# Two input transposes of a four-layer graph network moved from TensorE to VectorE blocks and DRAM, with a new instruction order

## The chip, the cores and the metric

The kernel runs on one core of a Trainium2 chip. The time is device microseconds of one execution; a run is compared with the kernel before on the same chip in the same rounds. The record marks an execution as slow when it is over 1.5% above the fastest of its kernel. In the lines of the profile PE is TensorE, PEld its weight loads, DVE VectorE, ACT ScalarE, POOL GpSimd and SP SyncE, whose queue (SPq) issues the DMAs; L480 is line 480 of that run's kernel, `x8` a count of instructions, and `<-` in brackets names what ended the wait before.

## The reference

The input is 32 graphs of 512 nodes with 256 features in fp32, and one 512 x 512 adjacency matrix shared by all. Four layers follow each other; each is `x = layernorm(x + layer(x))`.

```python
def reference(x, adj, ...):
    x = ln(x + L0(x))   # 8-head attention over adj, layernorm, FFN with relu, layernorm
    x = ln(x + L1(x))   # additive attention: softmax(leaky_relu(s1_i + s2_j) masked) @ (x W)
    x = ln(x + L2(x))   # softmax(leaky_relu((x W1)(x W2)^T) masked) @ (x W3), relu
    x = ln(x + L3(x))   # additive attention with 4 heads, elu
    return x            # ... cut: parameters, masks, constants
```

## The kernel before

A planner in the kernel's own Python decides the order of all instructions. Each operation has an assumed cost per engine; the planner starts what can start first and breaks ties by the age of the graph and the length of the work behind the operation. Every engine then executes its own list strictly in that order, so an instruction whose input is late holds everything behind it on its engine.

```python
AGE = 30.0
...
s, o, e = min((c for c in cands if c[0] <= tmin + 0.05),
              key=lambda c: (not c[1].frees, c[1].graph * AGE - c[1].rank))
...
plan = Plan(slots, {...}, 5, {"DVE": 1.0})      # five graphs in flight
```

The FFN of layer 0 and layer 2 need their input with features on the partitions. `transposed` did that on TensorE, eight 128 x 128 transposes into PSUM (the buffers that matmuls write, `ps` in the traces), copied out ("evicted") by ScalarE:

```python
def transposed(xs):
    xT = Buf("B")
    for s in range(2):
        ps = Buf("PS")
        def fn(e, s=s, ps=ps):
            for k in range(KC):
                for j in range(2):
                    nc.tensor.transpose(two(ps)[:, k, j * P:(j + 1) * P],
                                        T4(xs)[:, 2 * s + j, k * P:(k + 1) * P], ident)
        op({"PE": 4 * TR}, fn, r=[xs[s]], w=[ps], pre=[xT])
        evac(ps, xT, s, nodes(s), two)
    return xT
```

A layernorm works on half a graph at a time: statistics on VectorE, then four tiny steps on GpSimd (two columns each), then the scaling of the data on ScalarE:

```python
def layernorm(y, dst, ...):
    for s in halves:
        ...                                            # bn_stats, bn_aggr on VectorE -> mv
        def scales(e, mv=mv):
            m = mv.t[:, :4].rearrange("p (c k) -> p k c", k=2)
            nc.gpsimd.tensor_scalar(mv.t[:, 4:6], m[:, 1, :], 1.0, EPS, ALU.mult, ALU.add)
            nc.gpsimd.tensor_tensor(mv.t[:, 6:8], mv.t[:, 4:6], mhalf[:, :2], ALU.pow)
            nc.gpsimd.tensor_scalar(mv.t[:, 8:10], m[:, 0, :], -1.0, 0.0, ALU.mult, ALU.add)
            nc.gpsimd.tensor_tensor(mv.t[:, 10:12], mv.t[:, 8:10], mv.t[:, 6:8], ALU.mult)
        op({"POOL": 1.6}, scales, r=[mv], w=[mv])      # the planner assumes 1.6 us
        ...                                            # norm: ScalarE, x * scale + bias
```

## Time and profile before

| | before |
|---|---|
| median of the first 3 runs | 3023.44 us (3019.70 to 3026.94) |
| span of the trace | 3020.5 us |
| steady period per graph | 90.44 us, TensorE without a gap |
| span minus 32 periods (both ends) | 126.4 us |
| VectorE, ScalarE, DMA busy in a period | 81.7 us, 52.5 us, 12% |

The steady period is the distance of two equal instructions of neighbouring graphs in the trace. What is left of the span after 32 periods is what filling, draining and setup cost; I call it "the ends". The prediction shows the lines.

### The profile page before, as it was taken

The numbers are of one execution on the slowest core, as the hardware profiler recorded it, in microseconds if no ns is written. First come the engines' busy times: TensorE is split into PE (matmuls) and PEld (weight loads), VectorE is DVE, ScalarE is ACT, GpSimd is POOL, SyncE is SP. The second block draws the span as 40 slices with busy tenths as digits, with TensorE's granted clock in tenths as the row PEclk, the third lists the DMA queues.
The fourth block names the chain that finished last, engine by engine and source line by source line (L and its number), as shares of the span: only waits on it lengthen the run. The fifth ranks groups of instructions, "written<-read, shape, count | busy, mean of one in ns | idle before, by whom it ended". The sixth has DMA issues, their size and how long they took to land.

```text
span 3020.5 us, 49063 instructions
## 1 busy us (share of the span) xinstructions
PE 2947.4 (98%) x17898; PEld 1633.3 (54%) x17898; DVE 2635.2 (87%) x5277; ACT 1688.5 (56%) x3475; POOL 866.8 (29%) x1809
## 2 busy tenths in 40 slices
PE   8999999999999999999999999999999999999885
PEld 3465555555555555555555555555555555555452
DVE  7988899988899988899988899988899988889754
ACT  5546655665655665555665555665555665655432
POOL 0223322322322322322322322322322322322221
PEclk9999999999999999999999999999999999999997
DMA  7000110111110110110110110110110111110000
GB/s 139 12 19 22 39 39 19 40 39 22 39 39 19 39 40 22 39 39 18 40 40 22 39 39 19 40 39 22 39 39 19 40 39 24 37 32 19 32 25 29
DMA packets 194746, 102.67 MB, mean 34 GB/s; under 512 B 143937, under 2 KB 181313, under 8 KB 194497
## 3 DMA queue, kind: packets, MB, share of 16 engines
q1 hardware_dynamic: 193648, 97.63, 12.9%
q8 instruction: 142, 2.33, 0.3%
q10 hardware_dynamic: 848, 1.84, 0.2%
q14 instruction: 108, 0.88, 0.1%
HBM read 82.31 MB, written 17.12 MB: 33 GB/s over the span
## 4 chain that ended last, share of the span: by engine, by line
PE 92%; DVE 4%; issue 1%; DMA 1%; ACT 1%; POOL 1%; SPq 1%; DVEq 0%; ACTq 0%; POOLq 0%
PE ps L380 15%; PE ps L397 11%; PE ps L467 9%; PE ps L475 8%; PE ps L611 8%; PE ps L765 7%; PE ps L730 7%; PE ps L703 7%; PE ps L670 7%; PE ps L771 4%; PE ps L368 2%; PE ps L722 2%; PE ps L536 1%; PE ps L701 1%; PE ps L802 1%
## 5 line engine op out<-in xcount | busy, mean ns | idle before, releaser
L340 ACT ACTIVATE b<-ps 128x512 f32<-128x512 f32 x772 | 434.9, 602 | 497.2 <-PE ps L380 186.9
L486 DVE TENSOR_TENSOR b<-b,maskT 128x1024 f32<-128x1024 f32 x512 | 594.5, 1212 | 25.1 <-ACT b L480 25.1
L480 ACT ACTIVATE b<-ps 128x512 f32<-128x512 f32 x1024 | 528.4, 604 | 116.7 <-PE ps L475 116.7
L439 ACT ACTIVATE b<-b,t 128x256 f32<-128x256 f32 x768 | 425.6, 597 | 255.9 <-POOL t L430 244.3
L427 POOL TENSOR_SCALAR t<-t 128x2 f32<-128x2 f32 x384 | 135.2, 352 | 845.0 <-DVE t L422 777.8
L757 DVE SCALAR_TENSOR_TENSOR b<-b,s,maskT 128x512 f32<-128x512 f32 x512 | 358.7, 740 | 8.0 <-DMA b<-r 7.7
L428 POOL TENSOR_TENSOR t<-t,mhalf 128x2 f32<-128x2 f32 x384 | 340.0, 885 | 32.0
L475 PE MATMUL ps<-b,b 32*128 32x512 f32 x2048 | 300.4, 640 | 0.0
L498 DVE TENSOR_TENSOR b<-b,b 128x1024 f32<-128x1024 f32 x256 | 297.4, 1210 | 0.0
L420 DVE BATCH_NORM_STATS2 t<-b 128x6 f32<-128x256 f32 x768 | 284.4, 412 | 7.8 <-DVE b L580 0.5
L408 POOL TENSOR_TENSOR acc<-acc,s 128x32 f32<-128x32 f32 (+2 forms) x96 | 77.3, 806 | 637.8 <-DVE s L525 378.1
L467 PE MATMUL ps<-b,b 128*32 128x512 f32 x2048 | 250.9, 598 | 2.6 <-DVE b L486 2.3
L765 PE MATMUL ps<-b,b 128*64 128x512 f32 x1024 | 239.3, 606 | 13.1 <-DVE b L757 13.1
L380 PE MATMUL ps<-b,wqkv_sb 128*128 128x512 f32 x512 | 248.1, 609 | 0.0
L397 PE MATMUL ps<-w_sb,b 128*128 128x256 f32 x1024 | 245.6, 388 | 1.4 <-ACT b L340 1.4
L703 PE MATMUL ps<-b,b 128*128 128x512 f32 x512 | 240.6, 592 | 0.0
L380 PE MATMUL ps<-b,w_sb 128*128 128x512 f32 x512 | 235.5, 603 | 2.5 <-ACT b L340 2.5
L670 PE MATMUL ps<-b,b 128*128 128x257 f32 x1024 | 230.8, 383 | 2.5 <-issue 2.5
L730 PE MATMUL ps<-b,b 128*128 128x257 f32 x1024 | 228.5, 380 | 0.4 <-ACT b L340 0.4
L670 PEld LDWEIGHTS ps<-b,b 128*128 128x128 f32 x1024 | 195.8, 192 | 45.4 <-issue 10.6
L397 PEld LDWEIGHTS ps<-w_sb,b 128*128 128x128 f32 x1024 | 190.0, 191 | 53.8 <-issue 30.0
L408 POOL TENSOR_TENSOR acc<-acc,t 128x2 f32<-128x2 f32 (+2 forms) x128 | 37.9, 308 | 598.7 <-DVE t L789 325.7
(124 smaller groups left out, 4129.8 us busy)
## 6 DMA issues: line engine op xcount, KB each, us to landing
b<-r SPq DMA_DIRECT2D x64, 512.0 KB
b<-in_x_dram SPq DMA_DIRECT2D x128, 128.0 KB
b<-in_x_dram SPq DMA_DIRECT2D x32, 512.0 KB
out_dram<-b SPq DMA_DIRECT2D x64, 256.0 KB
b<-r SPq DMA_DIRECT2D x32, 256.0 KB
r<-s SPq DMA_DIRECT2D x128, 0.5 KB
r<-s SPq DMA_DIRECT2D x128, 2.0 KB
b<-in_adj_dram ACTq DMA_DIRECT2D x4, 256.0 KB
```

What stands on the lines that cost most here:

```text
L340: nc.scalar.activation(dst, src, AF.Copy)
L380: nc.tensor.matmul(ps.t, w.t[:, i, col + k * P:col + (k + 1) * P], T2(xT)[:, i, :], start=(i == 0), stop=(i == KC - 1))
L397: nc.tensor.matmul(two(ps)[:, j, :], T2(xT)[:, i, c * P:(c + 1) * P], w.t[:, i, col:col + C], start=(i == 0 and row is None), stop=(i == K ...
L439: nc.scalar.activation(o, i, AF.Identity, bias=b, scale=sc)
L467: nc.tensor.matmul(ps.t[D0 * h:D0 * h + D0, :], lhs(h), T2(p[h // 2][c])[:, h % 2, :], start=start, stop=stop)
L475: nc.tensor.matmul(s[h].t, T2(kT)[r:r + D0, g, c * P:(c + 1) * P], T2(qT)[r:r + D0, g, :], start=True, stop=True)
L480: op({"ACT": cact(512)}, lambda e, c=c, j=j, i=i, s=s, p=p: nc.scalar.activation(T2(p[j][c])[:, i, :], s[2 * j + i].t, AF.Exp, scale=SC0), ...
L486: nc.vector.tensor_tensor(t, t, maskT[c].t.unsqueeze(1).to_broadcast([P, 2, N]), ALU.mult)
L670: nc.tensor.matmul(ps.t[:, :C + 1], T2(p[m // 2])[:, m % 2, c * P:(c + 1) * P], hv.t[:, m * (C + 1):(m + 1) * (C + 1)], start=(m == 0), st ...
L703: nc.tensor.matmul(ps.t, T2(gT)[:, i, c * P:(c + 1) * P], T2(xT)[:, i, :], start=False, stop=(i == KC - 1))
L730: nc.tensor.matmul(ps_o.t[:, :C + 1], T2(pT)[:, j, m * P:(m + 1) * P], vv()[:, m, :], start=(m == 0), stop=(m == NC - 1))
L765: nc.tensor.matmul(ps_o[h // 2].t[D3 * (h % 2):D3 * (h % 2 + 1), :], T4(hv)[:, m + i, h * D3:(h + 1) * D3], T2(p[i][h // 2])[:, h % 2, :], ...
```

## The change

The intent is to take 16 transposes per graph off TensorE, the bounding engine. VectorE transposes 32 x 32 blocks, the half-done tile goes to DRAM in one write of 512 KB, and four reads of 128 KB bring the blocks back in their places. Because this takes longer, six graphs are kept in flight, the age step falls from 30 to 15, and the last two graphs get equal rank. The core of the diff:

```diff
-AGE = 30.0
+AGE = 15.0
+LAST = 2
...
-                          key=lambda c: (not c[1].frees, c[1].graph * AGE - c[1].rank))
+                          key=lambda c: (not c[1].frees, min(c[1].graph, len(self.graphs) - LAST) * AGE - c[1].rank))
...
-    plan = Plan(slots, {...}, 5,
+    plan = Plan(slots, {..., "E": [1] * 4, ...}, 6,
...
+    def quarters(xs):
+        xt = Buf("B")
+        for s in range(2):
+            op(TH, lambda e, s=s: nc.vector.transpose(
+                xt.t[:, :NC * C].rearrange("p (q c b) -> p c q b", c=NC, b=32)[:, 2 * s:2 * s + 2],
+                by_chunk(xs, s).rearrange("p c (q a) -> p c q a", a=32)),
+                r=[xs[s]], w=[xt[s]])
+        return xt
     def transposed(xs):
-        ... (TensorE transposes and evictions, shown above)
+        xt, xT, d = quarters(xs), Buf("B"), Buf("E")
+        op({"SP": DMA}, lambda e: nc.sync.dma_start(d.t, xt.t[:, :NC * C]), r=[xt], w=[d])
+        def get(e):
+            v = d.t.rearrange("(j a) (k i n) -> i a k j n", a=32, i=4, n=P)
+            for i in range(4):
+                nc.sync.dma_start(T2(xT)[32 * i:32 * i + 32].rearrange(
+                    "a k (j n) -> a k j n", n=P), v[i])
+        op({"SP": 4 * DMA}, get, r=[d], w=[xT])
         return xT
```

(The permuted node order is undone where the FFN's relu and layer 2's first product are evicted; layers 1 and 3 use `quarters` too, two half-tile transposes for four quarter-tile ones.)

More of the change, by code (lines that the diff above doesn't have):

```diff
@@ L291 @@
         "D": [tc.dram_tile([H3, N], FP, name=f"r{i}") for i in range(6)],
+        "E": [tc.dram_tile([P, NC * C], FP, name=f"e{i}") for i in range(6)],
         "PS": [psum.tile([P, N], FP, name=f"ps{i}") for i in range(8)],
@@ L297 @@
     nc.gpsimd.memset(ones, 1.0)
-    plan = Plan(slots, {"B": [14, 10, 10, 12], "S": [4] * 4, "T": [8] * 4, "D": [1] * 4, "PS": [0] * 4}, 5,
+    plan = Plan(slots, {"B": [14, 10, 10, 12], "S": [4] * 4, "T": [8] * 4, "D": [1] * 4, "E": [1] * 4, "PS": [0] * 4}, 6,
                 {"DVE": 1.0})
@@ L345, in evac @@
            r=[ps], w=[dst[part]])
-    def nodes(s):
-        return lambda b: T2(b)[:, :, s * 2 * P:(s + 1) * 2 * P]
     def swap(v):
@@ L357, in parts4 @@
         return v.rearrange("p (q i b) -> p q i b", q=NC, i=4)
-    def transposed(xs):
-        xT = Buf("B")
-        for s in range(2):
-            ps = Buf("PS")
-            def fn(e, s=s, ps=ps):
-                for k in range(KC):
-                    for j in range(2):
-                        nc.tensor.transpose(two(ps)[:, k, j * P:(j + 1) * P],
-                                            T4(xs)[:, 2 * s + j, k * P:(k + 1) * P], ident)
-            op({"PE": 4 * TR}, fn, r=[xs[s]], w=[ps], pre=[xT])
-            evac(ps, xT, s, nodes(s), two)
+    def quarters(xs):
[6 more added lines that the diff above has]
+        return xt
+    def transposed(xs):
+        xt, xT, d = quarters(xs), Buf("B"), Buf("E")
[6 more added lines that the diff above has]
+        op({"SP": 4 * DMA}, get, r=[d], w=[xT])
         return xT
@@ L383, in project_t, with project @@
         return ps
-    def project(xT, w, col, s, pre, row=None, part=None):
+    def project(xT, w, col, s, pre, row=None):
         ps = Buf("PS")
@@ L399, in fn @@
                                      stop=(i == KC - 1 and (row is None or j == 1)))
-        op({"PE": 2 * F + (0.1 if row is None else 0.33)}, fn, r=[xT[part], w] + ([row] if row else []),
+        op({"PE": 2 * F + (0.1 if row is None else 0.33)}, fn, r=[xT, w] + ([row] if row else []),
            w=[ps], pre=[pre])
@@ L560, in relu @@
             def relu(e, k=k, ps_h=ps_h):
-                o, i, b = T2(hT)[:, k, :], ps_h.t, b1_sb.t[:, k:k + 1]
+                o, i, b = swap(T2(hT)[:, k, :]), parts4(ps_h.t), b1_sb.t[:, k:k + 1]
                 if e == "ACT":
@@ L593, in scored @@
         R = [Buf("B") for _ in range(1 + (heads > 2))]
-        xt = Buf("B")
-        def xq():
-            return xt.t[:, :NC * C].rearrange("p (q c b) -> p c q b", c=NC, b=32)
-        for s in range(2):
-            for c in (2 * s, 2 * s + 1):
-                op({"DVE": cdve(256)}, lambda e, c=c: nc.vector.transpose(
-                    xq()[:, c], T4(xs)[:, c, :].rearrange("p (q a) -> p q a", a=32)),
-                    r=[xs[s]], w=[xt[s]])
+        xt = quarters(xs)
         pss = [Buf("PS") for _ in range(NC)]
@@ L685, in layer2 @@
         for k in range(KC):
-            evac(project_t(w12_sb, 0, xT, k, gT), gT, k, lambda b, k=k: T2(b)[:, k, :])
+            evac(project_t(w12_sb, 0, xT, k, gT), gT, k, lambda b, k=k: swap(T2(b)[:, k, :]),
+                 lambda b: parts4(b.t))
         def vv():
@@ L690, in layer2 @@
         for s in range(2):
-            evac(project(xT, w3_sb, 0, s, v, part=s), v, s, lambda b, s=s: vv()[:, 2 * s:2 * s + 2, :C], two)
+            evac(project(xT, w3_sb, 0, s, v), v, s, lambda b, s=s: vv()[:, 2 * s:2 * s + 2, :C], two)
         op({"DVE": 0.08}, lambda e: nc.vector.memset(vv()[:, :, C:C + 1], 1.0), r=[xT], w=[v])
@@ L859, in masks @@
             op({"DVE": 0.6}, lambda e, c=c: nc.vector.tensor_scalar(
-                swap(maskN.t[:, c, :]), parts4(edges(c)), 0.0, -BIG, ALU.is_le, ALU.mult),
+                maskN.t[:, c, :], edges(c), 0.0, -BIG, ALU.is_le, ALU.mult),
                 r=[f[c // 2][c % 2]], w=[maskN])
```

## The prediction

> **What bounds the kernel now.** I read the page first: busy shares, the 40 slices, the chain.
>
> ```profile
> PE 2947.4 (98%) x17898; PEld 1633.3 (54%) x17898; DVE 2635.2 (87%) x5277; ACT 1688.5 (56%) x3475; POOL 866.8 (29%) x1809
> ...
> PE   8999999999999999999999999999999999999885
> ...
> DVE  7988899988899988899988899988899988889754
> ...
> PE 92%; DVE 4%; issue 1%; DMA 1%; ACT 1%; POOL 1%; SPq 1%; DVEq 0%; ACTq 0%; POOLq 0%
> ```
>
> PE is busy almost everywhere, and 92% of the chain that ended last is PE. Gaps are only in the first and the last few slices. VectorE is second at 87%, and it too runs at 8 or 9 tenths for most of the program. Busy matmuls may still be stretched by waits, so I checked the rhythm. In the chain in order of time each layer-1 projection begins 90.44 us after the one before (1008.56, 1099.00, 1189.44 us), once per graph. The table of busy time by stretch over such a period:
>
> ```profile
> 1005.00:1095.44 90.44, 90.44 (x562) 50.15 (x558) 81.70 (x164) 52.48 (x109) 27.30 (x55) 1.00 0.12 33
> ```
>
> The columns are span, then busy time of PE, weight loads, VectorE, ScalarE and GpSimd, then clock, DMA share and GB/s. PE has no idle time in this period at clock 1.00, VectorE has 8.74 us of slack, DMA is 12% used. So in the middle the time is PE's work: 90.44 us per graph. 32 x 90.44 = 2894.1 us; the span is 3020.5, so 126.4 us are lost at head and tail (setup, filling, draining, slow clock). The last stretches of the same view:
>
> ```profile
> 2900.00:2960.00 60.00, 51.97 (x281) 31.80 (x274) 29.35 (x75) 21.29 (x47) 8.37 (x26) 0.91 0.09 32
> 2960.00:3020.50 60.50, 26.01 (x155) 12.55 (x153) 24.42 (x60) 8.40 (x19) 5.73 (x20) 0.74 0.09 28
> ```
>
> In the last 60 us PE works 26 us, at a clock of 0.74: the last graph runs layer 3 alone, its steps waiting for each other.
>
> **What the Trainium skill says.** (1) "VectorE: DVE Perf Modes", section The three transpose paths: VectorE transposes only 32x32 blocks, TensorE a full 128x128 into PSUM. That is why the change needs the trip through DRAM to regroup the blocks, and why the old path needs an eviction. The trace has both kinds: the block transposes of layer 0's input, and 128x128 TensorE transposes followed by ScalarE evictions. (2) "TensorE: Matmul & The Clock Gate", section PE-mode transpose, gives about 275 ns for a transpose in a kernel. The trace agrees (median 273 ns), but that is latency; transposes overlap, and the cost is their spacing, taken below. (3) "DMA: Bandwidth & Descriptors", section Anatomy of one DMA: about 2 us fixed plus bytes over 436 GB/s, fitted on another issuing path. For 512 KB that gives an estimate of 3.2 us each way. The trace before has no such round trip. Its 1 MB of loads for a new graph (issued from 1079.4 us) moved until about 1086 us at 140 to 230 GB/s in most microseconds, so I allow more. (4) "Perfetto Trace Analysis", section Identifying the Most-Contended Engine, warns that matmul busy time does not say how near PE is to its limit. It does not undo the argument here: what matters is that PE has no gap, and that removed instructions give back their spacing.
>
> **The change part by part.**
>
> *Removed from PE.* `transposed` is called twice per graph (FFN and layer 2), 8 transposes each: 16 per graph, 512 in all, which the groups view confirms:
>
> ```profile
> L368 PE MATMUL ps<-ident,b 128*128 128x128 f32 x512 | 71.8, 280 | 9.6 <-ACT b L439 9.5
> ```
>
> 512 x 280 ns would be 143 us, far too much, since they overlap. The timeline of PE in one period shows the true cost as the start of the group to the start of the next:
>
> ```profile
> 1046.39 1.03 PE L368 MATMUL ps<-ident,b 128*128 128x128 f32 x8
> 1047.36 1.14 PE L475 MATMUL ps<-b,b 32*128 32x512 f32 x8
> ...
> 1061.22 1.09 PE L368 MATMUL ps<-ident,b 128*128 128x128 f32 x8
> 1062.15 5.32 PE L380 MATMUL ps<-b,w_sb 128*128 128x512 f32 x12
> ```
>
> 0.97 + 0.93 = 1.90 us per graph, so the period falls to 88.54 us if PE stays full: 32 x 1.90 = 60.8 us, 2.01% of 3023.44. The chain's share of this line (1.9% of the span, 57 us) says the same. The intended gain alone lies exactly on the 2% line.
>
> *Removed from ScalarE.* 4 evictions of 512 columns per graph at 602 ns: 128 x 0.60 = 77 us. All those evictions run on ScalarE (its line has 772 of them, VectorE none). ScalarE is 58% busy in the period; nothing is gained. Two PSUM buffers fewer per call is a small relief.
>
> *Added to VectorE.* 4 half-tile block transposes per graph:
>
> ```profile
> L449 DVE STREAM_TRANSPOSE b<-b 128x512 f32<-128x512 f32 x64 | 42.0, 691 | 9.4 <-DMA b<-in_x_dram 9.4
> L602 DVE STREAM_TRANSPOSE b<-b 128x256 f32<-128x256 f32 x256 | 97.8, 417 | 6.2 <-ACT b L439 5.9
> ```
>
> Back to back, two of the first kind cover 1.30 us in the timeline, with overlap 0.61 us each: 4 x 0.61 = 2.44 us. In layers 1 and 3, 8 quarter transposes (1.41 us for four, some 0.34 each by spacing, 2.7 us) become 4 halves (2.44 us): minus 0.25. Net +2.2 us per graph: VectorE 81.7 + 2.2 = 83.9 us of an 88.54 us period, 95% instead of 90%. Still below PE, but its slack falls from 8.7 to 4.6 us.
>
> *Added on the DMA queue.* Per call one write of 512 KB (4 KB rows) and four reads of 128 KB (512-byte pieces): 10 more issues per graph on SP. At 0.4 to 0.8 us each (the issue lines of SP in the trace), that is 5 us on a queue that is mostly idle. Traffic: 64 x 0.5 = 33.5 MB written and as much read, 67 MB on top of 102.67 MB; DMA share 12% goes to some 17 to 20%. Bandwidth does not bind.
>
> *Moved: latency.* Transposed input used to be ready about 2 us after the layernorm (transposes from 1046.39, first projection at 1048.43). Now it takes VectorE 1.3 us, write 4 to 5 us, reads 5 to 6 us: an estimate of 11 to 12 us, twice per graph, some 20 us more. In the middle this is hidden if there are other graphs to run; that is what the sixth graph is for. With five graphs and a 90.44 us period a graph may stay up to 452 us; 20 us is under 5% of that. The extra tile life (two buffers of about 10 us, the layernorm result some 10 us longer, twice) is about 60 us of the 39 x 90.44 = 3527 buffer-us per period, under 2%. The buffer pool is not enlarged, but I expect it to suffice.
>
> *Order.* A smaller age step and equal rank for the last two graphs lets graphs 30 and 31 interleave to the end. The last 120 us before have PE busy for 78 us, so 42 us idle, and a slow clock in the rest. Two graphs in lockstep could fill maybe 10 to 20 us; the DRAM trips of the same two graphs, poorly covered there, and VectorE's added work in the filling stage (88% busy from 100 to 200 us) could take 5 to 15 us back. I choose a gain of about 6 us net.
>
> Sum: 32 x 88.54 = 2833.3; plus 126.4 for head and tail; minus 6; minus nothing for DMA, and 0 for stalls: 2953.7. The measured times lie up to 3 us above the span of the trace, and I round down a little for the lighter PSUM use: I say **2952 us**, 2.4% faster.
>
> **Rivals.** (a) *VectorE becomes the bound, or nearly.* At 95% with dependences both ways, PE may wait in each period. For: head stretches where VectorE is 88% busy show PE at 92%. Against: at 90% in the steady middle PE has zero idle time, as the static order interleaves well. If PE waited 1 us per graph: +32 us, about 2984, within 2%.
> (b) *The wait moves to the DMA trip.* SP takes its instructions in order; a read that waits for its write's landing holds back the score rows of layers 1 and 3 and the next input. For: in the tail VectorE already waited 7.7 us for such rows. Against: those rows are needed only by queued VectorE work, and SP's issues fill under 13 of 90 us. If it bites in every graph, PE stalls 1 to 3 us per period and the whole gain is gone: 2985 to 3040.
> (c) *The order is the larger effect.* If the sixth graph and the shared rank drain the tail well, 30 of the 126 us could go: about 2930, over 3% faster. If they starve the oldest graph of buffers, the tail lengthens: 2975.
> (d) *The transposes were hidden anyway.* Against: zero PE idle in the middle, and the line in the chain; I give it 3%.
>
> **Range and chances.** The sure term is 61 us; the rest is the two ends (plus or minus 20) and stalls (0 to 40, more likely near 0). 80% range: 2922 to 2992. The line for "faster by over 2%" is 2963; my centre is 11 us below it. Faster 0.60, within 2% 0.36, slower by over 2% 0.04.
>
> **What would show each step.** In the changed trace: no 128x128 transposes of the FFN's and layer 2's input, PE records down by 512; the period between layer-1 projections 88.5 us with PE fully busy (right), or above 89.5 us with PE idle on VectorE results or on loads from DRAM (a or b). VectorE 83 to 85 us busy per period; ScalarE down 2.4 us; DMA share 17 to 20%; write to last read's landing around 10 us, with PE not named as waiting for it. Last 120 us: PE idle under 42 us. The prediction is wrong if PE shows idle time in every period, if PE's remaining matmuls get longer or fall to a lower clock, or if the ends change by more than 30 us.

## The result

The changed kernel takes **2985.06 us** (median of 4 runs, 2981.72 to 2990.92) against 3022.16 us of the kernel before in the same rounds. The ratio is 0.9877, with a 95% interval of 0.9855 to 0.9900: 1.2% faster, within 2%. Here and below a ratio is the mean time of one kernel's fast runs over that of the other's of the same rounds, so it is not quite the ratio of the medians that I quote.

The page after: the busy line, the row of TensorE's 40 slices and the chain that ended last.

```profile
PE 2899.7 (97%) x17376; PEld 1600.0 (54%) x17386; DVE 2682.6 (90%) x5277; ACT 1623.4 (54%) x3347; POOL 779.4 (26%) x1809
...
PE   8999999999999999999999999999999999999994
...
PE 70%; issue 11%; DVE 11%; POOL 4%; DMA 2%; ACT 1%; SPq 1%; DVEq 0%; POOLq 0%; ACTq 0%
```

The 512 transposes are gone (weight loads fell from 17898 to 17386), but TensorE's share of the chain fell from 92% to 70%, and GpSimd's rose from 1% to 4%. The slices still show 9 throughout the middle: a loss of one or two per cent is invisible in tenths. It shows in the rhythm. The order now repeats every three graphs; the busy table of one such period (columns as in the prediction):

```profile
1019.43:1289.40 269.97, 267.06 (x1630) 148.69 (x1630) 249.69 (x486) 151.18 (x313) 72.38 (x165) 0.99 0.22 57
```

That is 89.99 us per graph; from 1217.26 to 2571.51 us, 15 graphs, the average is 90.28 us. Before it was 90.44. So the middle, where 1.90 us per graph should have been won, won almost nothing. TensorE now has 2.9 us without work per period, and the mean clock is 0.99. VectorE is busy 249.69 / 3 = 83.2 us per graph. The table of waits of TensorE names the idle time (total us, times, longest):

```profile
PE ps L480 <- ACT b L342: 20.0, 9, 2.5
PE ps L762 <- DVE b L754: 18.4, 3, 15.1
...
PE ps L386 <- DVE b L454: 6.1, 9, 0.7
...
PE ps L386 <- DMA b<-e: 0.2, 1, 0.2
```

The first wait comes nine times, once every three graphs, 2.2 us on average. L480 is the product of queries and keys in layer 0, L342 the eviction of those queries and keys by ScalarE. (The second wait is the last graph's layer 3 at the very end.) The DRAM trips, `b<-e`, cost TensorE 0.2 us in the whole run. The timeline around one of these waits, first TensorE, then ScalarE:

```profile
1260.98 1.92 PE L472 MATMUL ps<-b,b 128*32 128x512 f32 x16
1265.08 2.58 PE L480 MATMUL ps<-b,b 32*128 32x512 f32 x8 [2.18 <-ACT b L342]
1267.59 5.40 PE L386 MATMUL ps<-b,w_sb 128*128 128x512 f32 x8
1272.92 3.79 PE L607 MATMUL ps<-l1w_sb,b 32*128 32x259 f32 x64
```

```profile
1258.92 1.09 ACT L444 ACTIVATE b<-b,t 128x256 f32<-128x256 f32 x2 [3.66 <-POOL t L435]
1263.46 1.09 ACT L444 ACTIVATE b<-b,t 128x256 f32<-128x256 f32 x2 [3.45 <-POOL t L435]
1264.46 1.54 ACT L342 ACTIVATE b<-ps 128x512 f32<-128x512 f32 x3
```

The evictions (L342) did not wait for TensorE: they stood in ScalarE's list behind the scaling of a layernorm (L444), which waited 3.45 us for GpSimd. GpSimd and VectorE at that time:

```profile
1256.54 1.20 POOL L434 TENSOR_SCALAR t<-t 128x2 f32<-128x2 f32 x1
1257.83 1.06 POOL L435 TENSOR_TENSOR t<-t 128x2 f32<-128x2 f32 x1
1258.97 1.05 POOL L432 TENSOR_SCALAR t<-t 128x2 f32<-128x2 f32 x1
1260.10 1.55 POOL L433 TENSOR_TENSOR t<-t,mhalf 128x2 f32<-128x2 f32 x1
1261.62 0.66 POOL L434 TENSOR_SCALAR t<-t 128x2 f32<-128x2 f32 x1
1262.37 1.06 POOL L435 TENSOR_TENSOR t<-t 128x2 f32<-128x2 f32 x1
```

```profile
1256.48 2.35 DVE L491 TENSOR_TENSOR b<-b,maskT 128x1024 f32<-128x1024 f32 x2
1258.74 2.36 DVE L503 TENSOR_TENSOR b<-b,b 128x1024 f32<-128x1024 f32 x2
1261.02 2.35 DVE L507 TENSOR_TENSOR b<-b,b 128x1024 f32<-128x1024 f32 x2
```

GpSimd's steps on two columns have medians of 0.19 us (0.69 us for the power), but here they take 0.66 to 1.55 us. Four steps need 4.46 us (1258.97 to 1263.43) where the planner assumed 1.6. They run beside VectorE instructions that read two tiles, and in the single records five of the six steps shown end 0.05 to 0.06 us after one of those VectorE instructions has ended; the sixth, the power, ends 0.55 us after one. The Trainium skill, "SBUF — State Buffer", section SBUF: two separate sides, says that VectorE and GpSimd share one port pair, held for a whole instruction by a VectorE instruction with two SBUF inputs, and that the other then blocks. The trace fits; experiments below test it.

The stall costs more than itself. First, the eight matmuls of L480 took 2.51 us from their start to that of the next group, where 1.07 us is usual. The clock was still at 1.00. In the single records their pairs start 0.48 us apart, each 0.05 us after the end of a ScalarE instruction (1265.03, 1265.51, 1266.00 and 1266.49 us): TensorE goes on waiting for ScalarE, but the table counts this as busy. Then the clock falls. The busy table in stretches of 1 us (the third column from the end is the clock):

```profile
1267.00:1268.00 1.00, 1.00 (x4) 0.35 (x2) 0.99 (x1) 1.00 (x3) 0.00 (x0) 0.89 0.00 0
1268.00:1269.00 1.00, 1.00 (x2) 0.34 (x1) 1.00 (x2) 1.00 (x3) 0.00 (x0) 0.50 0.00 0
...
1271.00:1272.00 1.00, 1.00 (x4) 0.51 (x3) 1.00 (x2) 0.69 (x1) 0.00 (x0) 0.90 0.00 0
```

Some 2.7 us after work resumed the clock is halved, for 3.4 us, and the eight of L386 take 5.33 us where some 3.6 is usual. The skill, "TensorE: Matmul & The Clock Gate", section Part 1: The HAM clock gate, describes windows of 3.4 us after which an idle TensorE runs at half clock. In the trace's clock record every one of the nine stalls is followed by such a dip: three last 3.4 us and six 6.8 us, and between 300 and 2700 us there is no other. The two groups lose 1.4 and 1.7 us. With 2.18 + 0.67 us of waits, this period loses 6.0 us, or 2.0 per graph, and TensorE counts as busy in half of that. From 300 to 2700 us TensorE was idle for 26.2 us and at half clock for 51.2, about half of which is lost: some 52 us in 26.6 graphs, or 1.95 per graph.

The DRAM trip itself was shorter than I had estimated. The issues of one trip on the DMA queue:

```profile
1244.35 0.33 SPq L370 DMA_DIRECT2D e<-b  x1
1246.96 2.53 SPq L375 DMA_DIRECT2D b<-e  x4
```

The traffic of the reads ends at about 1251.3 us in the busy table by microsecond, 7 us after the write was issued.

The ends got shorter: 2989.1 - 32 x 90.28 = 100 us, against 126. (The traced run is the slowest of the four, 6 us above the median, so up to 6 us of the 100 may be scatter.) The stretches from 200 to 100 us before the end, before and after, show part of it. Before:

```profile
2820.50:2920.50 100.00, 83.56 (x479) 52.62 (x472) 63.38 (x158) 32.33 (x72) 19.30 (x56) 0.88 0.09 31
```

After:

```profile
2789.10:2889.10 100.00, 99.28 (x584) 64.82 (x577) 67.83 (x179) 50.26 (x105) 21.72 (x59) 1.00 0.18 59
```

TensorE works 99 of these 100 us at full clock instead of 84 at 0.88.

### The profile page after: what moved, and what is told of

Its sections match the earlier page's. It is cut to its first block, busy times and chain, and to the rows that moved or that the text cites. A ratio compares the mean times of both kernels' runs of the same rounds, so it can differ in the third digit from the quotient of the medians.

```text
span 2989.1 us, 48564 instructions
## 1 busy us (share of the span) xinstructions
PE 2899.7 (97%) x17376; PEld 1600.0 (54%) x17386; DVE 2682.6 (90%) x5277; ACT 1623.4 (54%) x3347; POOL 779.4 (26%) x1809
## 4 chain that ended last, share of the span: by engine, by line
PE 70%; issue 11%; DVE 11%; POOL 4%; DMA 2%; ACT 1%; SPq 1%; DVEq 0%; POOLq 0%; ACTq 0%
PE ps L386 12%; PE ps L402 8%; PE ps L472 7%; PE ps L700 7%; PE ps L607 7%; PE ps L666 7%; PE ps L480 6%; PE ps L762 5%; PE ps L727 4%; PE ps L768 3%; DVE b L491 2%; DVE t L425 2%; POOL t L433 2%; POOL t L435 1%; POOL t L434 1%
## 5 line engine op out<-in xcount | busy, mean ns | idle before, releaser
L491 DVE TENSOR_TENSOR b<-b,maskT 128x1024 f32<-128x1024 f32 x512 | 597.9, 1218 | 56.5 <-ACT b L485 56.5
L485 ACT ACTIVATE b<-ps 128x512 f32<-128x512 f32 x1024 | 522.5, 619 | 170.6 <-PE ps L480 169.9
L444 ACT ACTIVATE b<-b,t 128x256 f32<-128x256 f32 x768 | 422.1, 602 | 348.5 <-POOL t L435 337.2
L342 ACT ACTIVATE b<-ps 128x512 f32<-128x512 f32 (+1 forms) x644 | 364.7, 605 | 413.0 <-PE ps L386 153.5
L432 POOL TENSOR_SCALAR t<-t 128x2 f32<-128x2 f32 x384 | 127.5, 332 | 1567.2 <-DVE t L427 1459.8
L754 DVE SCALAR_TENSOR_TENSOR b<-b,s,maskT 128x512 f32<-128x512 f32 x512 | 345.9, 745 | 38.5 <-DMA b<-r 38.4
L480 PE MATMUL ps<-b,b 32*128 32x512 f32 x2048 | 302.6, 639 | 22.6 <-ACT b L342 20.0
L433 POOL TENSOR_TENSOR t<-t,mhalf 128x2 f32<-128x2 f32 x384 | 308.6, 804 | 32.0
L503 DVE TENSOR_TENSOR b<-b,b 128x1024 f32<-128x1024 f32 x256 | 303.2, 1220 | 3.0 <-PE ps L472 3.0
L472 PE MATMUL ps<-b,b 128*32 128x512 f32 x2048 | 263.1, 603 | 5.6 <-DVE b L491 4.4
L386 PE MATMUL ps<-b,w_sb 128*128 128x512 f32 x512 | 258.1, 644 | 0.2 <-DMA b<-e 0.2
L386 PE MATMUL ps<-b,wqkv_sb 128*128 128x512 f32 x512 | 230.1, 601 | 6.1 <-DVE b L454 6.1
L666 PEld LDWEIGHTS ps<-b,b 128*128 128x128 f32 x1024 | 193.3, 189 | 37.1 <-issue 9.8
L727 PEld LDWEIGHTS ps<-b,b 128*128 128x128 f32 x1024 | 190.7, 189 | 36.3 <-ACT b L485 7.6
L480 PEld LDWEIGHTS ps<-b,b 32*128 32x128 f32 x2048 | 105.8, 185 | 183.4 <-issue 80.8
```

Source lines behind the costliest of these rows:

```text
L386: nc.tensor.matmul(ps.t, w.t[:, i, col + k * P:col + (k + 1) * P], T2(xT)[:, i, :], start=(i == 0), stop=(i == KC - 1))
L444: nc.scalar.activation(o, i, AF.Identity, bias=b, scale=sc)
L472: nc.tensor.matmul(ps.t[D0 * h:D0 * h + D0, :], lhs(h), T2(p[h // 2][c])[:, h % 2, :], start=start, stop=stop)
L480: nc.tensor.matmul(s[h].t, T2(kT)[r:r + D0, g, c * P:(c + 1) * P], T2(qT)[r:r + D0, g, :], start=True, stop=True)
L485: op({"ACT": cact(512)}, lambda e, c=c, j=j, i=i, s=s, p=p: nc.scalar.activation(T2(p[j][c])[:, i, :], s[2 * j + i].t, AF.Exp, scale=SC0), ...
L491: nc.vector.tensor_tensor(t, t, maskT[c].t.unsqueeze(1).to_broadcast([P, 2, N]), ALU.mult)
```

## The experiments

Twelve kernels ran, with three rounds each. Theory A: the order that the planner makes for the changed kernel puts evictions behind a layernorm whose GpSimd steps are slow beside VectorE, and the loss in the middle is that. Rivals: VectorE's load, the DRAM trips, or a change of the ends.

| run | median us | ratio to before | period us | ends us |
|---|---|---|---|---|
| changed kernel | 2985.06 | 0.9877 | 90.28 | 100 |
| e1 order alone | 2993.82 | 0.9905 | 90.71 | 89 |
| e2 DRAM transposes alone | 3018.60 | 0.9986 | 89.62 | 150 |
| e3 planner's GpSimd cost 4.0 | 3317.48 | 1.0976 | not even | |
| e4 two GpSimd steps (wrong result) | 2926.19 | 0.9683 | 88.22 | 99 |
| e5 three GpSimd steps | 2939.00 | 0.9721 | 89.07 | 92 |
| e6 before, two GpSimd steps (wrong result) | 3013.09 | 0.9969 | 90.44 | 116 |
| e7 five in flight | 3083.68 | 1.0195 | 93.8 | |
| e8 lighter VectorE | 2979.03 | 0.9855 | 90.29 | 88 |
| e9 one-input additions (wrong result) | 2936.73 | 0.9719 | 88.59 | 99 |
| e10 before, shared rank | 3023.64 | 1.0007 | 90.44 | 127 |
| e11 before, age step and six | 2987.45 | 0.9889 | 90.71 | 81 |
| e12 e5 without shared rank | 2944.62 | 0.9742 | 88.77 | 103 |

Periods are read off the moments when results are stored (averages over up to 15 graphs), the ends are the span minus 32 periods. Both come from one traced execution each, and executions of a kernel differ by up to 0.3% (9 us for the changed kernel), so differences of a few us between ends say little. ScalarE's list is the same, compared by operation and tile, in the changed kernel, e4, e5, e8 and e9.

### e1: the order alone

```diff
 (kernel before)
-AGE = 30.0
+AGE = 15.0
+LAST = 2
-  key: c[1].graph * AGE - c[1].rank
+  key: min(c[1].graph, len(self.graphs) - LAST) * AGE - c[1].rank
-  plan = Plan(slots, {...}, 5,
+  plan = Plan(slots, {...}, 6,
```

> TensorE transposes as in the kernel before; only the age step of 15, the shared rank of the last two graphs and six graphs in flight are taken over. Theory A (the loss of the change is in the new order, which puts ScalarE evictions behind layernorms that wait for GpSimd, once per three graphs): this kernel keeps all of before's PE work, so it cannot fall under about 3000 us; if its order has such stalls too it lands at 3020 to 3060 with dips of the granted clock in the middle of the run, if not at 3005 to 3020. Rival B (the loss comes from the trips through DRAM or from VectorE's extra transposes): no PE idle time in the middle, 3000 to 3020 us.

It took 2993.82 us: 28 of the 37 us that the whole change won. That is under the floor that I had given for theory A, which missed that the ends could win 37 us. The middle has no stall:

```profile
1201.70:1292.41 90.71, 90.71 (x559) 50.13 (x558) 81.27 (x163) 52.47 (x109) 20.85 (x56) 1.00 0.12 33
```

So the new order (age step, sixth graph and shared rank together) makes the ends better and, with TensorE transposes, brings no stall.

### e2: the DRAM transposes alone

```diff
 (changed kernel)
-AGE = 15.0
-LAST = 2
+AGE = 30.0
-  key: min(c[1].graph, len(self.graphs) - LAST) * AGE - c[1].rank
+  key: c[1].graph * AGE - c[1].rank
-  plan = Plan(slots, {...}, 6,
+  plan = Plan(slots, {...}, 5,
```

> VectorE block transposes and trips through DRAM as in the changed kernel, but the age step of 30, no shared rank and five graphs in flight as before. Theory A (the stall belongs to the order): the order differs, so the stall of 2.2 us per three graphs may be gone; without it 32 x 88 us of PE work plus the 126 us that the two ends cost before is about 2940 us. Rival B (the trips or VectorE's load stall PE): PE idle in the middle on loads from DRAM or on VectorE, 2980 us or more. Rival C (the sixth graph is needed to hide the trips): 3000 us or more, with waits for the DRAM copy.

It took 3018.60 us, no gain. A period of two graphs:

```profile
1178.88:1358.10 179.22, 178.38 (x1086) 97.62 (x1085) 166.30 (x325) 99.19 (x209) 51.55 (x111) 1.00 0.21 57
```

The middle wins 0.82 us per graph, 26 us in all; TensorE is idle for 0.4 us per graph. Its work is 89.2 us per graph and not 88.5. Why was not followed; one possible reason is that the lists interleave kinds of matmuls differently (in the changed kernel, a group of eight of L480 takes 1.07 us alone and two in a row take 1.93 us). But the ends grew from 126 to 150 us. There TensorE waits 9.6 us for the blocks to transpose, 7.7 us on DRAM reads and 8.7 us for layer 1's attention weights in the last 320 us. The trips are hidden in the middle and not at the ends. (In the middle there was one wait of 2.76 us for VectorE's blocks, with a dip of the clock after it.) No named theory was quite right; rival B and C saw the number, but it was the ends.

### e3: a truer GpSimd cost for the planner

```diff
 (changed kernel)
-        op({"POOL": 1.6}, scales, r=[mv], w=[mv])
+        op({"POOL": 4.0}, scales, r=[mv], w=[mv])
```

> The changed kernel with one number of the planner changed: GpSimd's four steps of a layernorm half are taken to cost 4.0 us instead of 1.6, near the 3.3 to 4.5 us that the trace shows where VectorE runs two-input instructions beside them. Instructions stay the same, only their order changes. Theory A: the planner no longer puts evictions behind norms that are not ready; PE idle time in the middle goes from 26 us to under 8, the clock stays at 1.00, 2925 to 2950 us. Rival B (VectorE at 92% or the DRAM trips cause the loss): no gain, 2975 to 3000 us.

A clear miss: 3317.48 us. The instructions are the same, but the new order makes TensorE wait for the DRAM trips:

```profile
PE ps L386 <- DMA b<-e: 260.9, 27, 14.7
```

In one of these waits (602.88 us, 14.66 us long) VectorE's blocks were done at 589.7. The write was issued at 591.29, after four other DMAs of the same queue; the reads went out from 595.35, after seven more; and they ended at 602.74. The trip took 11.5 us, and TensorE's list had nothing to do in between. This shows that the rival of the DRAM trips is real in a less lucky order. It says nothing against theory A, for in this order the old stall is gone; it says that correcting one constant of a greedy planner is not a controlled experiment.

### e4: the same order, a shorter GpSimd chain

```diff
 (changed kernel)
-            nc.gpsimd.tensor_scalar(mv.t[:, 4:6], m[:, 1, :], 1.0, EPS, ALU.mult, ALU.add)
-            nc.gpsimd.tensor_tensor(mv.t[:, 6:8], mv.t[:, 4:6], mhalf[:, :2], ALU.pow)
-            nc.gpsimd.tensor_scalar(mv.t[:, 8:10], m[:, 0, :], -1.0, 0.0, ALU.mult, ALU.add)
-            nc.gpsimd.tensor_tensor(mv.t[:, 10:12], mv.t[:, 8:10], mv.t[:, 6:8], ALU.mult)
+            nc.gpsimd.tensor_tensor(mv.t[:, 6:8], m[:, 1, :], mhalf[:, :2], ALU.pow)
+            nc.gpsimd.tensor_tensor(mv.t[:, 10:12], m[:, 0, :], mv.t[:, 6:8], ALU.mult)
```

> The changed kernel in exactly its own order (the planner's costs are kept), but GpSimd does two steps per layernorm half instead of four; the sign of the mean term and the small constant are left out, so the result is wrong on purpose. Theory A (the stall is ScalarE's queue waiting for GpSimd's chain): the chain of two halves falls from about 7.8 to about 4 us, the periodic PE stall of 2.2 us and the slow clock after it vanish, 2930 to 2950 us. Rival B (VectorE's load or the DRAM trips): VectorE and DMA are untouched, so 2980 to 2990 us as the changed kernel.

It took 2926.19 us, 59 us under the changed kernel and 4 us under the range for theory A, with the planner's costs and so the order kept. Its output is wrong, which doesn't matter for the time. The stall and the slow clock are gone:

```profile
1191.43:1456.10 264.67, 264.45 (x1628) 147.26 (x1627) 249.38 (x487) 150.81 (x312) 47.34 (x94) 1.00 0.22 58
```

TensorE is idle 0.2 us in three graphs, with VectorE busy as before (249.38 against 249.69 us) and the DRAM trips as before. Its work is then 88.2 us per graph: without the stall the transposes are worth about 2.2 us per graph, more than the 1.90 that I had measured. That the different order is the reason is likely but not shown; e9 below gives 1.85.

### e5: a version with a right result

```diff
 (changed kernel; signs is a constant tile of -1, 1, -1, 1)
+            nc.gpsimd.tensor_tensor(mv.t[:, 12:16], mv.t[:, :4], signs, ALU.mult)
+            m = mv.t[:, 12:16].rearrange("p (c k) -> p k c", k=2)
+            nc.gpsimd.tensor_tensor(mv.t[:, 6:8], m[:, 1, :], mhalf[:, :2], ALU.pow)
+            nc.gpsimd.tensor_tensor(mv.t[:, 10:12], m[:, 0, :], mv.t[:, 6:8], ALU.mult)
 (in place of the four steps)
```

> The changed kernel in its own order, GpSimd with three steps per layernorm half instead of four and a right sign (mean and variance are multiplied by -1 and 1 in one step; the small constant 1e-5 is left out, an error of some 5e-6 relative, so the result should pass). Theory A (GpSimd's chain holds ScalarE's queue): the chain of two halves gets about 2 us shorter, which is nearly the whole stall of 2.2 us; 2930 to 2955 us, most of what two steps gave (2926). Rival B (two steps were faster for another reason, such as the wrong values): 2975 to 2990 us.

It took 2939.00 us with a right result: 2.8% faster than the kernel before (0.9721, interval 0.9705 to 0.9737), and faster than the changed kernel. It leaves out the small constant of the layernorm (1e-5), which these inputs do not need; a kernel for any input would have to keep it.

### e6: the control

```diff
 (kernel before)
 (the same two steps as in e4 in place of the four)
```

> Control: the kernel before in its own order with the two-step GpSimd chain (wrong result on purpose, as in the run with two steps). Theory A: before has no PE idle time in its middle, so a shorter chain is worth nothing there and only a few us at the two ends: 3008 to 3022 us. Rival B (a shorter GpSimd chain helps VectorE or ScalarE everywhere, whatever the order): as large a gain as in the changed kernel, about 59 us, so 2955 to 2975 us.

It took 3013.09 us: 10 us less, with the period at 90.44 us as before. The shorter chain is worth 10 us at the ends of the old order. So most of the 59 us of e4 belong to the stall of the changed kernel; up to about 10 may be a gain that any order has.

### e7: five graphs in flight

```diff
 (changed kernel)
-  plan = Plan(slots, {...}, 6,
+  plan = Plan(slots, {...}, 5,
```

> The changed kernel with five graphs in flight instead of six; the age step of 15 and the shared rank stay. If the sixth graph is what hides the DRAM trips: PE waits for loads from DRAM or for the blocks to transpose, 3000 us or more. If the smaller age step does it (graphs less spread out, two near each other at the end): within 15 us of the changed kernel, 2970 to 3000 us.

It took 3083.68 us. With the small age step, five graphs give a period of about 93.8 us, and TensorE is idle for 80 us between 300 and 2700 us. The largest of these waits, 26.5 us in seven, is for VectorE's blocks before the projections of layers 1 and 3, which take no DRAM trip; the trips themselves account for 5.9 us, and the rest is spread over small waits for VectorE and ScalarE. With this age step the sixth graph is needed, but not for the DRAM trips alone (e2, with the old step, ran five graphs at 89.62). Why this order is so poor stays open.

### e8: less work on VectorE

```diff
 (changed kernel, costs in the planner kept)
-  three tensor_tensor per half graph: xs + be2 (zero), u * g1 (ones), y2 * g2 (ones)
+  left out
```

> The changed kernel in its own order, but VectorE leaves out the two multiplications by layernorm gains of one and the addition of a bias of zero, six half-tile instructions or about 3.6 us per graph, more than the 2.2 us net that the change added; with these inputs the result stays right. GpSimd's four steps stay. If only the length of GpSimd's chain matters: the stall stays, 2965 to 2988 us. If VectorE's load is the cause or a part of it (it reaches the statistics late, so the chain starts late): the stall goes as well, 2920 to 2945 us.

It took 2979.03 us. VectorE fell from 83.2 to 79.8 us per graph, more than the change had added, yet the period stayed at 90.29 and the stall came again, nine times, eight of them with a dip of the clock. The timeline of TensorE shows one:

```profile
1257.91 3.53 PE L480 MATMUL ps<-b,b 32*128 32x512 f32 x8 [2.48 <-ACT b L342]
```

VectorE's load is not the cause. The 6 us by which this run is faster are no more than the spread of the changed kernel's own runs (2981.72 to 2990.92 us).

### e9: the same load without a second input

```diff
 (changed kernel; the 12 additions per graph that sum layer 0's weights)
-  nc.vector.tensor_tensor(T2(a), T2(a), T2(b), ALU.add)
+  nc.vector.transpose(T2(a), T2(b))
```

> The changed kernel in its own order; the 12 additions per graph that sum the weights of layer 0 (two SBUF inputs, 1.22 us each) are replaced by block transposes of the same size, which read one input (0.69 us for half the width, so about 1.2 us). Wrong on purpose. GpSimd keeps its four steps. If GpSimd's steps are held while VectorE runs an instruction with two SBUF inputs: the chain's second half, now beside one-input instructions, falls from 4.5 to about 1.6 us, the stall of 2.2 us per three graphs goes, 2925 to 2950 us. If GpSimd's steps are slow for another reason (waiting for events, VectorE's mere load): no change, 2975 to 2990 us.

It took 2936.73 us. Its output is wrong, which doesn't matter for the time. The replaced instructions take as long as the additions did (1219 against 1220 ns), GpSimd still has four steps, the order is the same, and the stall is gone. The GpSimd chain at that place, from the last two steps of the first half:

```profile
1236.82 1.20 POOL L434 TENSOR_SCALAR t<-t 128x2 f32<-128x2 f32 x1
1238.10 1.05 POOL L435 TENSOR_TENSOR t<-t 128x2 f32<-128x2 f32 x1
1239.24 0.19 POOL L432 TENSOR_SCALAR t<-t 128x2 f32<-128x2 f32 x1
1239.51 0.69 POOL L433 TENSOR_TENSOR t<-t,mhalf 128x2 f32<-128x2 f32 x1
1240.17 0.19 POOL L434 TENSOR_SCALAR t<-t 128x2 f32<-128x2 f32 x1
1240.45 0.19 POOL L435 TENSOR_TENSOR t<-t 128x2 f32<-128x2 f32 x1
```

The second half takes 1.4 us instead of 4.46. The two steps before it still fall beside two-input instructions that the edit left (L491), and still take 1.20 and 1.05 us. So GpSimd is held by VectorE instructions with two inputs, as the skill's page says, and that made the stall.

### e10 and e11: which part of the order made the ends better

```diff
 (e10: kernel before with LAST = 2 and its key, age step 30, five graphs)
 (e11: kernel before with the age step of 15 and six graphs, old key)
```

> The kernel before with nothing but the shared rank of the last two graphs. The middle must stay at 90.44 us per graph. If the shared rank makes the better ends (the order alone gave 28 us): 2990 to 3005 us. If the age step and the sixth graph make them: 3012 to 3024 us.

> The kernel before with the age step of 15 and six graphs, without the shared rank. The counterpart of the last run: 2990 to 3005 us if these two make the ends better, 3015 to 3030 us (the middle is then 90.70 us per graph, 8 us more in all) if the shared rank does.

e10 took 3023.64 us, nothing won. e11 took 2987.45 us, with ends of 81 us. The age step and the sixth graph make the ends better. The shared rank does nothing in the old order, and with the new one it may cost some 6 us (e1 against e11, in different rounds; the intervals of their ratios overlap). e11 has no DRAM trips and no stall, and its ratio, 0.9889, is the changed kernel's 0.9877 within the noise: two numbers of the planner give what the whole change gave. The two were not tried apart from each other on the kernel before.

### e12: a candidate

```diff
 (e5)
-LAST = 2
-  key: min(c[1].graph, len(self.graphs) - LAST) * AGE - c[1].rank
+  key: c[1].graph * AGE - c[1].rank
```

> Candidate: the changed kernel with three GpSimd steps and without the shared rank of the last two graphs (age step of 15 and six graphs kept). The shared rank gave nothing alone, and leaving it out seemed to give 6 us where TensorE transposes: if that carries over, 2925 to 2938 us, under the 2939 us of three steps alone; if the two DRAM trips of the last graphs need the shared rank, 2940 to 2960 us.

The hope failed: 2944.62 us, in the range of the other branch and a little over e5. ScalarE's lists of e5 and e12 are the same until about 2718 us, so the 0.3 us per graph between their periods is scatter. From the store of the 26th graph to the end e12 takes 325.5 us and e5 319.7. So with the DRAM trips the last graphs seem to profit from the shared rank, by some 6 us; the intervals of the two ratios overlap. e5 remains the fastest version with a right result that ran.

## Why the prediction was right or wrong

The measured time lies in the range, and the outcome, within 2%, was given 0.36 where "faster" was given 0.60. The centre, 2952 us, was 33 us too low. Two of the prediction's own signs of being wrong came true: PE has idle time in every period (2.9 us in three graphs), and its clock falls to 0.50 after each stall. Term by term:

- **What bounds it: right.** TensorE's work sets the middle: in every version without stalls the period equals TensorE's busy time (90.71 in e1, 88.2 in e4).
- **TensorE saves 1.90 us per graph: right.** Once nothing stalls, it is 1.85 us in e9 (90.44 to 88.59) and 2.2 in e4 (to 88.22), or 2.5 against the 90.71 of the new order.
- **"0 for stalls": the step that failed.** The runs showed 1.7 to 2.1 us per graph in its place (90.28 less the 88.59 of e9 or the 88.22 of e4), 54 to 66 us over 32 graphs, which took back nearly all of the gain of the middle. The path is ScalarE's list, held by a layernorm whose GpSimd steps wait for VectorE's two-input instructions, and then the halved clock. Zero idle time in the old order says nothing of a new order, and I did not ask what each list would wait for in the new one. The new order and the DRAM transposes have no such periodic stall when each is alone (e1, e2); what in their combination puts the evictions behind that layernorm was not followed.
- **"A gain of about 6 us net" at the ends: the second failed term, of the other sign.** The ends won 26 us (126 to 100). The order wins 37 us there with TensorE transposes (e1), and the DRAM trips cost 24 us in the old order (e2) and about 11 in the new (e1 to the changed kernel, up to 6 of it scatter). I had said 10 to 20 and 5 to 15. The reason I gave was wrong as well: the shared rank did nothing (e10), the age step with the sixth graph did it (e11).
- **Rival (a), VectorE as the bound: wrong in its cause, right in its size by luck.** I set its worth at 1 us per graph, and PE was idle for 0.97, but with the slow clock and the hidden waits the loss was twice that, and VectorE's load is not why (e8). What VectorE does to GpSimd is (e9). Its busy time, 83.2 us per graph, was predicted as 83.9.
- **Rival (b), the DRAM trip: not in this order.** The trip takes 7 us, or 8.3 with the transposes, where I had said 11 to 12, and TensorE waited for it 0.2 us. In e3's order it cost 261 us.
- **Rival (c), the order as the larger effect: right.** Alone it makes 28 us of the 37 (36 without the shared rank, e11), while the transposes alone make under 4.
- **Smaller things.** DMA share: 22% where I said 17 to 20. DRAM traffic: plus 67 MB, as said. ScalarE: 50.4 us per graph, 2.1 less, where I said 2.4. PE idle in the last 120 us: 38.5, under the 42 as said.

With e4's figures the sum is 2953.7 + 66 for stalls - 20 at the ends - 10 for a middle of 88.22 and not 88.54 = 2989.7, and the traced run has 2989.1. Two errors of opposite sign brought the time into the range; that is luck as much as width.

## What to carry to other kernels

When lists are static, ask of a change what it does to the order, and test the order alone: here it gave most of the gain, or all of it (e11), and in combination with the new transposes it also brought the stall. Follow a wait of the bounding engine back through the list of the engine that it names, since the instruction named (an eviction) may only stand behind the culprit (a layernorm waiting for GpSimd). Tiny GpSimd steps in a critical chain should be few, or kept away from long VectorE instructions with two inputs.

## What the Trainium skill lacked or had wrong

- "TensorE: Matmul & The Clock Gate": it puts the fall to half clock after about 3.4 us of idle time. Here nine waits of 1.8 to 2.5 us were each followed by 3.4 or 6.8 us at a clock of 0.50, beginning 0.1 to 2.9 us after work had resumed; one of 1.98 us in e8 was not. Waits of 0.67 us had no such effect.
- "SBUF — State Buffer": the lock is described rightly; it gives no cost for small GpSimd steps. Four two-column steps took 4.46 us beside two-input VectorE instructions and 1.4 us beside one-input ones of the same length.
- "VectorE: DVE Perf Modes": the three transpose paths have no row for blocks regrouped through DRAM. Here the VectorE part of a 512 x 256 fp32 tile is two instructions of 0.69 us and the trip takes 7 us with free queues, 11.5 us behind other DMAs; the same on TensorE cost 0.95 us and two evictions of 0.60 us.
- "TensorEngine Tiling (Array Packing)": it gives no time for a change from one kind of matmul to another. Here eight matmuls of L480 took 1.07 us between other kinds, and sixteen in a row 1.93 us.
